# A one-byte memset on GpSimd after each gather of a two-layer graph network

## The chip, the cores and the metric

The kernel runs on one core of a Trainium2 chip. The metric is the device time of one execution in microseconds. A profile of one execution is given with it; its engines are PE (TensorE's matmuls), PEld (TensorE's weight loads), DVE (VectorE), ACT (ScalarE), POOL (GpSimd) and SP (SyncE, which here only issues DMAs).

## The reference

A relational graph convolution with two layers runs over 12,500 nodes of 128 features and 200,000 edges that are sorted by their destination. Each edge has one of 8 types. In each layer every edge takes its source node's row through its type's 128 x 128 matrix; the messages of one destination and type are averaged, the averages summed over the types, and `x @ root + bias` added. A relu and the layer's input follow. At the end the first input is added and a layer norm taken.

```python
def _rgcn_conv(x, src, dst, et, basis, comp, root, bias):
    W = jnp.einsum('rb,bio->rio', comp, basis)
    xw = jnp.einsum('ni,rio->nro', x, W)
    msgs = xw[src, et]
    seg = dst * N_REL + et
    summed = jax.ops.segment_sum(msgs, seg, num_segments=N_NODES * N_REL)
    cnt = jax.ops.segment_sum(jnp.ones((msgs.shape[0],), x.dtype), seg, num_segments=N_NODES * N_REL)
    mean = summed / jnp.maximum(cnt, 1.0)[:, None]
    agg = mean.reshape(N_NODES, N_REL, HIDDEN).sum(axis=1)
    return agg + x @ root + bias
...
for l in range(N_LAYERS):
    h_new = jax.nn.relu(_rgcn_conv(h, src, dst, edge_type, basis[l], comp[l], root[l], bias[l]))
    h = h_new + h
...
x = _layernorm(x + h, axis=-1)
```

## The kernel before

The edges are cut into T = 1563 tiles of 128. A *quad* is Q = 4 tiles (391 quads in a layer), a *group* is 8 tiles. One indirect DMA on GpSimd (`gather`, line 577) fetches the 128 source rows of one tile from HBM, 64 KB, into a quarter of a `rows` buffer. The `rows` buffers form a ring of AHEAD + 2 = 14 quads, so 56 gathers fit; the loop issues the gathers of quad q + 12 when it writes the code of quad q.

In layer 1 the rows come from `x`. For each quad VectorE builds one-hot matrices `dm` weighted with the inverse counts (`onehot`, line 863), TensorE multiplies `rows` by `dm` into `s` (`means`, line 903), and ScalarE copies `s` from PSUM to `sT` (line 565 is the helper of all its copies). Each group then goes through the eight type matrices into `y` (`product`, line 927), ScalarE copies that to `ys`, and TensorE puts it in its place (`place`, line 950). A finished block of 128 nodes is turned and multiplied by all eight matrices of layer 2 (`close_block`, lines 963 to 975), and SP stores the products to `y_d`.

In layer 2 the rows come ready multiplied from `y_d`. So a quad needs only `dm` and one product per tile, accumulated in PSUM over the quads of a block (`add_rows`, line 1016). `finish` and `norm` (lines 1028 to 1057) add bias, relu, residual and layer norm on VectorE and ScalarE, and SP stores the block. Layer 2's first gather waits for the last store of `y_d`. At the start of layer 1 VectorE and TensorE also count the edges of each destination and type (`counts`, lines 699 to 706).

A planner (`Plan`) takes the operations in the order written and gives each engine its waits on semaphores. Each engine runs its own operations in that order. A quad's gathers wait for TensorE to have used the ring's buffer 14 quads before, and for the quad three before to have landed, since the quads take turns on three DMA semaphores (`"gq": 3`). TensorE's products wait for the landing and for `dm`. A second, general path in the file runs only if the edges do not fit the assumptions of the first; it does not run here.

Of the kernel before, what the change touches and what calls it, by code (L numbers as in the profile page):

```python
# [415 lines left out]
def ordered_path(  # L416
# [24 lines left out]
    nc = tc.nc  # L441
    P = 128
    N, D = x.shape
    E = src.shape[0]
    L, NB = basis.shape[0], basis.shape[1]
# [3 lines left out]
    T = -(-E // P)  # L449
# [4 lines left out]
    Q = 4  # L454
# [16 lines left out]
    def keep(shape, dtype, name):  # L471
        return const.tile(shape, dtype, name=name)

    hT_d = dram.tile([NT * P, P], F32, name="hT_d")
    y_d = dram.tile([N * R, D], F32, name="y_d")
# [28 lines left out]
    sel = keep([P, G, K], F32, "sel")  # L504
    spread = keep([P, B, GB], F32, "spread")

    key = keep([P, 4, C], F16, "key")
    low = keep([P, 4, C], I32, "low")
    eqs = Ring(const, 2, [P, S4, 4, C], F16, "eq")
# [59 lines left out]
    def gather(l, q):  # L569
        if q >= NQ:  # L570
            return
        t, cell = rows_r.take()
        rows_g[l, q] = (t, cell)
        ids = idx if l == 0 else idy

        def emit():
            return [nc.gpsimd.indirect_dma_start(  # L577
                out=t[:, i - q * Q, :], out_offset=None, in_=x if l == 0 else y_d,
                in_offset=bass.IndirectOffsetOnAxis(ap=ids[:, i:i + 1], axis=0))
                for i in range(q * Q, min((q + 1) * Q, T))]  # L580

        b = q * Q // P
        reads = ["idx0" if l == 0 and q == 0 else ("idx", b)] if l == 0 else [("idy", b)]
        if l == 1 and q == 0:
            reads += [("y_d", j) for j in range(NT)]
        plan.add("POOL", emit, reads, [cell], lane="gq", n=min(Q, T - q * Q))
# [590 lines left out]
@with_exitstack  # L1177
def kernel(
    ctx: ExitStack,
    tc: tile.TileContext,  # L1180
    x: bass.AP,
    src: bass.AP,
    dst: bass.AP,
    et: bass.AP,
    basis: bass.AP,
    comp: bass.AP,
    root: bass.AP,
    bias: bass.AP,
    out: bass.AP,
):  # L1190

    nc = tc.nc
    flag = ctx.enter_context(tc.tile_pool(name="flag", bufs=1))
    bad = flag.tile([1, 1], I32, name="bad")
    ordered_path(tc, bad, x, src, dst, et, basis, comp, root, bias, out)
    redo = nc.values_load(bad, min_val=0, max_val=P_MAX)  # L1200
    with tc.If(redo > 0):
        general_path(tc, x, src, dst, et, basis, comp, root, bias, out)
# [27 lines left out]
```

## Time and profile before

| | |
|---|---|
| median of 3 runs | 4643.5 us (4638.13 to 4643.62) |
| the profiled execution's own time | 4641.11 us |
| its span in the profile | 4639.3 us |
| busy: PE, PEld, DVE, ACT, POOL | 51%, 41%, 37%, 11%, 64% |
| gathers | 3126: layer 1 starts from 3.4 to 2327.4 us, layer 2 from 2379.7 to 4590.5 us |
| DMA packets | all queues together took 22% of the 16 engines, mean 64 GB/s |
| granted TensorE clock, mean | 0.776 |

A line of the profile's groups gives the source line, the engine, the operation, what it writes and reads and how often; then the busy time in us and the mean length of one in ns; then the engine's idle time ahead of these instructions and what ended most of it. "Issue" there is time in which the engine waited for nothing that the profile shows, and "remote" is a wait whose end the profile can't ascribe to an instruction. A line of the list of waits gives the total in us, the number of waits and the longest. A line of the timeline gives the start in us, the length in us, the engine, the line and the operation; behind it in brackets stands the idle time ahead of it. TensorE runs each float32 matmul in two records, so a quad's four products are eight records.

### The profile page before, as it was taken

To read this page: it belongs to the slowest core of one execution; us is meant where nothing else is said; L and a number is where in the kernel's file an instruction comes from. 1 tells how busy PE (TensorE), PEld (TensorE's weight loads), DVE (VectorE), ACT (ScalarE), POOL (GpSimd) and SP (SyncE) were. 2 spreads that over 40 slices of the span, in tenths; PEclk is the share of its full clock that TensorE was granted. 3 is DMA by queue.
4 is the path that set the end of the run, shared out by engine and by line. 5 is a ranking of instruction groups with operands and counts; after the bars stand their busy time and mean duration, and the time that the engine had idled before them with its cause. 6 is when DMAs were issued, how large, how long until landed. Compare 5 with 4: busy or idle time off the path is not lost.

```text
span 4639.3 us, 34983 instructions
## 1 busy us (share of the span) xinstructions
PE 2355.8 (51%) x11691; PEld 1911.0 (41%) x11691; DVE 1697.2 (37%) x4724; ACT 502.0 (11%) x1190; POOL 2962.0 (64%) x3134
## 2 busy tenths in 40 slices
PE   1675565556655565565563443444444344444444
PEld 1454555455544554454442332333333233333333
DVE  3874222222222232232232343434334343434434
ACT  0121111111111111121110000000000000000000
POOL 5466666666666666666646666666666666666663
PEclk9998888788788877788876776777777776767677
DMA  2122222222222222222221111211111111111121
GB/s 79 37 71 74 75 75 74 74 75 75 74 74 74 75 79 73 72 79 74 70 69 51 55 56 54 57 55 56 54 56 56 55 56 56 54 55 56 54 57 37
DMA packets 193392, 295.75 MB, mean 64 GB/s; under 512 B 60725, under 2 KB 130687, under 8 KB 193203
## 3 DMA queue, kind: packets, MB, share of 16 engines
q0 software_dynamic: 100032, 205.07, 15.6%
q1 hardware_dynamic: 90650, 86.62, 5.8%
q8 instruction: 96, 1.57, 0.1%
q10 hardware_dynamic: 2521, 1.73, 0.1%
q14 instruction: 93, 0.76, 0.1%
HBM read 229.18 MB, written 64.00 MB: 63 GB/s over the span
## 4 chain that ended last, share of the span: by engine, by line
another core or an unknown queue 38%; PE 26%; DVE 17%; issue 14%; ACT 3%; POOL 2%; DMA 0%; POOLq 0%; DVEq 0%; ACTq 0%; SPq 0%
DVE dm L863 12%; PE s L903 8%; PE y L927 6%; PE pt L975 4%; PE po L950 3%; POOL rows L577 2%; PE s L1016 1%; ACT sT L565 1%; DVE w_sb L597 1%; PE ct L705 1%; DVE eq L699 1%; PE ct L706 1%; DVE st L1052 1%; DVE ys L1057 1%
## 5 line engine op out<-in xcount | busy, mean ns | idle before, releaser
L577 POOL DMA_INDIRECT rows<-in_x_dram,idx x1563 | 1485.4, 950 | 841.0 <-issue 420.5
L577 POOL DMA_INDIRECT rows<-y_d,idy x1563 | 1475.5, 944 | 787.6 <-issue 419.0
L1016 PE MATMUL s<-dm,rows 128*128 128x256 f32 x2086 | 646.0, 469 | 595.1 <-DVE dm L863 482.0
L863 DVE TENSOR_SCALAR dm<-cols,near,w 128x256 f32<-128x256 f32 x1563 | 727.0, 533 | 255.3 <-remote 185.9
L1016 PEld LDWEIGHTS s<-dm,rows 128*128 128x128 f32 x2086 | 487.6, 245 | 710.3 <-DVE dm L863 499.6
L863 DVE TENSOR_SCALAR dm<-cols,kr,w 128x128 f32<-128x128 f32 x1563 | 525.9, 401 | 569.3 <-remote 348.1
L903 PEld LDWEIGHTS s<-dm,rows 128*128 128x128 f32 x3126 | 470.9, 222 | 121.9 <-issue 115.4
L903 PE MATMUL s<-dm,rows 128*128 128x128 f32 x3126 | 485.5, 305 | 6.1 <-issue 5.1
L950 PE MATMUL po<-ys,pl 128*128 128x128 f32 x780 | 167.6, 349 | 628.3 <-ACT ys L565 467.6
L927 PE MATMUL y<-w_sb,sT 128*128 128x128 f32 x3136 | 439.5, 300 | 65.4 <-issue 43.3
L1016 PE MATMUL ct<-dm,rows 128*128 128x256 f32 x1040 | 314.6, 457 | 291.1 <-DVE dm L863 216.7
L927 PEld LDWEIGHTS y<-w_sb,sT 128*128 128x128 f32 x3136 | 422.8, 216 | 75.1 <-issue 48.8
L950 PEld LDWEIGHTS po<-ys,pl 128*128 128x128 f32 x780 | 131.1, 239 | 656.4 <-ACT ys L565 486.9
L1016 PEld LDWEIGHTS ct<-dm,rows 128*128 128x128 f32 x1040 | 235.2, 237 | 347.7 <-DVE dm L863 224.7
L963 DVE TENSOR_TENSOR h<-po,bias_sb 128x128 f32<-128x128 f32 x98 | 28.5, 291 | 872.3 <-PE s L903 281.2
L1051 DVE TENSOR_TENSOR h<-po,xs 128x128 f32<-128x128 f32 x98 | 27.9, 285 | 816.6 <-remote 731.7
L565 ACT ACTIVATE sT<-s 128x512 f32<-128x512 f32 x391 | 233.8, 598 | 838.5 <-PE s L903 466.3
L975 PE MATMUL pt<-w_sb,y_col 128*128 128x512 f32 x392 | 254.1, 736 | 55.2 <-issue 31.2
L1050 PE MATMUL po<-ident,y_col 128*128 128x128 f32 x98 | 37.5, 383 | 379.8 <-DVE y_col L1036 185.3
L1050 PEld LDWEIGHTS po<-ident,y_col 128*128 128x128 f32 x98 | 15.4, 157 | 415.2 <-DVE y_col L1036 205.8
L1054 ACT ACTIVATE st<-st,eps 128x1 f32<-128x1 f32 x98 | 28.9, 294 | 1187.8 <-DVE st L1053 931.6
L565 ACT ACTIVATE y_row<-pt 128x512 f32<-128x512 f32 x196 | 117.0, 597 | 215.0 <-PE pt L975 95.2
(120 smaller groups left out, 1148.9 us busy)
## 6 DMA issues: line engine op xcount, KB each, us to landing
y_d<-y_row SPq DMA_DIRECT2D x97, 512.0 KB
rows<-in_x_dram,idx POOLq DMA_INDIRECT x1563
rows<-y_d,idy POOLq DMA_INDIRECT x1563
h_in<-in_x_dram SPq DMA_DIRECT2D x98, 64.0 KB
h_in<-hT_d SPq DMA_DIRECT2D x98, 64.0 KB
xs<-in_x_dram SPq DMA_DIRECT2D x98, 64.0 KB
hT_d<-y_col SPq DMA_DIRECT2D x97, 64.0 KB
out_dram<-ys SPq DMA_DIRECT2D x97, 64.0 KB
```

The source lines that it names most:

```text
L565: act(lambda: nc.scalar.activation(out_t, in_t, AF.Copy), reads, writes)
L577: return [nc.gpsimd.indirect_dma_start(out=t[:, i - q * Q, :], out_offset=None, in_=x if l == 0 else y_d, in_offset=bass.IndirectOffsetOnA ...
L597: vec(lambda b=b: nc.vector.scalar_tensor_tensor(w_sb[:, l, r, :], b_sb[:, l, b, :], comp_sb[:, c0 + b:c0 + b + 1], w_sb[:, l, r, :], op0= ...
L699: vec(lambda s=s, eq=eq, s0=s0: nc.vector.tensor_tensor(eq[:, s - s0, :nb, HALO - s:HALO + P], key[:, :nb, HALO - s:HALO + P], key[:, :nb, ...
L705: nc.tensor.matmul(ct[:, :nb, :], id_h, eq[:, s - s0, :nb, main], start=(s == 1), stop=False)
L863: last = nc.vector.tensor_scalar(t[:, i - q * Q, :wide], cols[:, :wide], ids[:, i:i + 1], w[:, i:i + 1], op0=ALU.is_equal, op1=ALU.mult)
L903: last = nc.tensor.matmul(s[:, i, :], t[:, i, :], d[:, i, :P], start=True, stop=True)
L927: last = nc.tensor.matmul(y[:m], t[:, r, :nt, :].rearrange("p t k -> p (t k)"), w_sb[:, 0, r, :], start=(r == 0), stop=(r == R - 1))
L950: last = nc.tensor.matmul(po[j][0][:n], t[:m, k * P:k * P + n], o[:m], start=False, stop=(j in closed))
L975: pe(lambda: nc.tensor.matmul(pt[:n].rearrange("p r d -> p (r d)"), yc[:, :n], w_sb[:, 1, k * H:(k + 1) * H, :].rearrange("p r d -> p (r d)"),
L1016: ins = nc.tensor.matmul(a, t[:, i, :], d[:, i, :], start=(opens and i == 0), stop=(last and i == n - 1))
L1050: pe(lambda: nc.tensor.transpose(p[:n, :], v[:, :n], ident), [vc, "ident"], [pc])
```

## The change

A scratch tile `pace` of one byte per partition and gather is added. After each gather, GpSimd clears that gather's byte in all 128 partitions. The planner still sees only the gathers: the memset has no wait and signals nobody.

```diff
+    pace = keep([P, L * T], mybir.dt.uint8, "pace")
...
         def emit():
-            return [nc.gpsimd.indirect_dma_start(
-                out=t[:, i - q * Q, :], out_offset=None, in_=x if l == 0 else y_d,
-                in_offset=bass.IndirectOffsetOnAxis(ap=ids[:, i:i + 1], axis=0))
-                for i in range(q * Q, min((q + 1) * Q, T))]
+            ins = []
+            for i in range(q * Q, min((q + 1) * Q, T)):
+                ins.append(nc.gpsimd.indirect_dma_start(
+                    out=t[:, i - q * Q, :], out_offset=None, in_=x if l == 0 else y_d,
+                    in_offset=bass.IndirectOffsetOnAxis(ap=ids[:, i:i + 1], axis=0)))
+                nc.gpsimd.memset(pace[:, l * T + i:l * T + i + 1], 0)
+            return ins
```

## The prediction

> **What bounds the kernel now.** I read the costliest groups first. GpSimd issues 3126 gathers, 1563 per layer:
>
> ```profile
> L577 POOL DMA_INDIRECT rows<-in_x_dram,idx x1563 | 1485.4, 950 | 841.0 <-issue 420.5 <-PE s L903 195.9 <-remote 186.9
> L577 POOL DMA_INDIRECT rows<-y_d,idy x1563 | 1475.5, 944 | 787.6 <-issue 419.0 <-remote 243.0 <-DMA y_d<-y_row 51.4
> ```
>
> A gather is busy for 0.944 us, and half of the idle time ahead of it is "issue", which is no wait: GpSimd's timeline has the next gather 0.30 us after the last one's end, so the undisturbed beat is 1.249 us. 3126 x 1.249 = 3904 us of the 4639.3 us span. No other engine is busy for more than 51%, so the rest is not somebody else's work; it is pauses of this chain. By first and last starts (3.4 and 2327.4 us; 2379.7 and 4590.5 us) layer 1 takes 2324.0 us where 1562 beats are 1951, layer 2 takes 2210.8. So 373 us of pauses lie in layer 1, 260 in layer 2; beside them stand 3.4 us at the start, 51 between the layers and 48 after the last gather. Of the 373, 103 fall before 331 us, where only 180 gathers were issued and VectorE is 70 to 80% busy counting edges. About 530 us of pauses are left for the steady part.
>
> GpSimd's list of waits tells for whom it pauses:
>
> ```profile
> POOL rows L577 <- remote: 429.9, 145, 11.3
> POOL rows L577 <- PE s L903: 195.9, 74, 31.4
> ```
>
> The wait is the one for TensorE to free the `rows` buffer of 14 quads ago. So TensorE seems late. But a window without gathers (between the layers) says that it is not slow. Here are ScalarE's copies of `s`, one per quad, with the gathers and without; the columns are the stretch, its length, ScalarE's busy time and count, the clock, the DMA share:
>
> ```profile
> 350.00:2320.00 1970.00, 203.77 (x341) 0.81 0.25 74
> 2332.00:2376.00 44.00, 7.06 (x12) 0.97 0.19 70
> ```
>
> With gathers a quad takes 1970 / 341 = 5.78 us. Without them 44 / 12 = 3.67, where four gathers need 5.0. What holds TensorE up is seen in the timeline of all engines:
>
> ```profile
> 1503.19 0.94 POOL L577 DMA_INDIRECT rows<-in_x_dram,idx  x1 [0.30 <-issue]
> 1503.63 0.27 PE L903 MATMUL s<-dm,rows 128*128 128x128 f32 x1 [0.27 <-issue]
> 1506.48 0.60 ACT L565 ACTIVATE sT<-s 128x512 f32<-128x512 f32 x1 [5.08 <-remote]
> 1506.71 0.94 POOL L577 DMA_INDIRECT rows<-in_x_dram,idx  x1 [2.58 <-remote]
> ```
>
> TensorE's last product of the quad ends at 1503.9 us; ScalarE, idle, may copy it only at 1506.48, 2.6 us later and 2.3 us after GpSimd fell silent. GpSimd's own wait, also for TensorE, ends 0.2 us after that. The start of the program shows the same with no ring and no gathered data in play: VectorE's comparison waits for TensorE while gathers stream without a break.
>
> ```profile
> 51.30 0.69 DVE L699 TENSOR_TENSOR eq<-key 128x157 f16<-128x157 f16 x4 [20.95 <-remote]
> ```
>
> So my reading is: **while gathers follow each other at 1.25 us, TensorE's completions reach the other engines late, often only when GpSimd pauses; the ring then fills, GpSimd pauses, and everything comes free.** GpSimd's beat is the floor; these late completions are what stands on top of it. Why they are late, the trace does not say.
>
> **What the Trainium skill says.** "Perfetto Trace Analysis", section "GPSIMD Engine Instruction", advises timing GpSimd's instructions by start-to-start spacing and not by the reported span. The trace agrees: the only memsets of 128x1 that GpSimd runs are reported with 99 to 119 ns and start 30 ns apart:
>
> ```profile
> 0.30 0.11 POOL L1216 MEMSET const-bfloat16-1.0<- 128x1 bf16 x1
> 0.33 0.12 POOL L1216 MEMSET const-uint8-127<- 128x1 uint8 x1
> ```
>
> "GPSIMD Engine Reference", section "2.1 Instruction dispatch": completion of an instruction holds back who waits on its semaphore, not the next GpSimd instruction. The memset has no semaphore, so by this the next gather need not await its write; these overlapping memsets agree. "SBUF — State Buffer", section "Who interferes with whom": a VectorE instruction with two SBUF inputs contends with a GpSimd instruction that reads SBUF, not with one that only writes. A memset only writes; whether it collides, no run here shows. "Perfetto Trace Analysis", section "Tensor Engine Instruction": TensorE's reported end is estimated and its semaphore follows PSUM's acknowledgement. So a late completion could be real work behind a modelled end. Against that stands the window between the layers, where ScalarE's 11 waits for `s` come to 5.1 us in all.
>
> **The change part by part.** It removes and moves nothing: the compiled order of PE, DVE, ACT and SP is the same instruction by instruction, and no wait is added. It adds 3126 memsets on GpSimd, each behind a gather. Behind each stands the next gather; VectorE, ScalarE and SP do not wait for it. The new tile is written by nobody else.
>
> Price of one, d. Lower bound 0.03 us (the spacing). Upper bound 0.40 us: its 0.10 us, and a gap of 0.30 of its own as between two gathers. I take 0.10 us, its reported length, since nothing overlaps a gather here today and a memset would run in the gap at best. A beat becomes 1.349 us. There are 2 x 1562 = 3124 beats, so 312 us more on GpSimd.
>
> It lies beside the pauses, of which there are 633 us; it is hidden only as far as these shrink. If completions come in time, the sum is: 3124 x 1.349 = 4214; start, middle and end 3.4 + 51 + 48 = 102; start-up pauses 103 less the 180 x 0.10 = 18 that the longer beat eats, 85; a tenth of the steady pauses left, 53, as I do not expect all to go. That is 4454 us. Less some of the middle and the end, which now hold up to 14 quads of backlog: 11 fewer quads at 3.67 us (layer 1) and at 2.2 us (layer 2, 90 matmul records of 8 per quad in 25 us after the last gather) would save 64; I count half, 32. So 4422 us of span. The profiled execution took 4641.1 us, its span 4639.3, and the median of the three runs is 4643.5, 4 us above the span: **about 4430 us**, 4.6% less. Late next would be GpSimd itself, with TensorE a few quads behind it.
>
> The step that I can't derive is that 0.10 us between gathers is enough. For it: the lateness is seen only in streams of gathers at the short beat, and completions within a stream do get through, some after 1 us and some after 14 us, so it is a matter of chance slots and not a lock; and the steady pauses of 530 us are worth more than 312. Against it: within a stream most beats let none through, and a memset keeps GpSimd as busy as before.
>
> **The rivals.**
> 1. *The holds stay and the beat adds up (slower).* If completions still come mainly in the pauses, each turn of the ring, 12 gathers and a pause of 2.6 us (1506.71 to 1524.07 us), gets 12 x 0.10 longer and its pause stays. Then 4643.5 + 312 - 18 = 4938 us. For it: at the pause of 1521.4 us the same 2.4 us pass before TensorE is heard. Against it: 3.67 us per quad as soon as gathers stop. It decides if under 312 of the 633 us of pauses go.
> 2. *The memset is dear (slower).* With no steady pauses at all, GpSimd alone reaches today's span where 102 + 85 + 3124 x (1.249 + d) = 4639, that is at d = 0.176 us. At the upper bound of 0.40 it is 102 + 85 + 3124 x 1.649 = 5339 us. For it: the constant 0.30 us between gathers could be a cost of every instruction there. Against it: the 30 ns between memsets, and iotas that start 0.08 to 0.31 us apart without such a gap.
> 3. *No change.* Either the memset runs inside the 0.30 us and the beat stays (it doesn't do what it says), or holds last a fixed time and the pauses shrink by just what the beats gain: 4640 us.
>
> **How the numbers follow.** A measurement of this kernel can tell about 0.2% (9 us) from no change. Forecast 0.52, rival 1 0.27, rival 2 0.13, rival 3 0.08. Faster 0.52, same 0.08, slower 0.40. Low end: the forecast at d = 0.03 is 3124 x 0.07 = 219 less, 4211; I put 4220. High end: rival 1 at d = 0.13 is 4643.5 + 406 - 23 = 5027; 5050 leaves out most of rival 2 and the dear end of rival 1, some 0.15. Where the signs split so, the likeliest case's own range is 4220 to 4600.
>
> **What would show it.** Right: GpSimd's starts 1.33 to 1.37 us apart in both layers; its waits for TensorE and "remote" down from 626 us to under 150; ScalarE's copies of `sT` and VectorE's L1051 without waits of 5 us and more; the gathers of a layer spread over some 2110 to 2230 us. Wrong: a start-to-start of 1.45 us or more (rival 2); pauses of 2.6 us that still come every 8 to 12 gathers behind the longer beat (rival 1); starts still 1.25 us apart (rival 3).

## The result, and the profile after

The change makes no gain: 4655.8 us after (median of 10 runs, 4652.7 to 4662.1) against 4645.4 us before (10 runs, 4636.7 to 4650.7), a ratio of 1.0024 with a 95% interval of 1.0015 to 1.0034. Faster by 4.6% was forecast; it is slower by a quarter of a per cent. The memset is there, 3126 times, and the beat is what it was.

These are the costliest groups of GpSimd in the profile after (busy us, mean ns, idle time ahead and what ended it). Lines of the kernel have moved by 3 or 4 against those of before:

```profile
L580 POOL DMA_INDIRECT rows<-in_x_dram,idx x1563 | 1488.1, 952 | 659.5 <-issue 268.9
L580 POOL DMA_INDIRECT rows<-y_d,idy x1563 | 1476.8, 945 | 612.6 <-issue 296.5
L583 POOL MEMSET pace<- 128x1 uint8 x3126 | 375.0, 120 | 4.2 <-issue 2.5
```

The memsets are busy for 375 us, the 312 us of the forecast and more. But the "issue" ahead of the gathers fell from 839.5 us (420.5 + 419.0) to 565.4. The memset took the place of idle time. GpSimd's timeline shows how (start, length, and in brackets the idle time ahead):

```profile
1502.47 0.94 POOL L580 DMA_INDIRECT rows<-in_x_dram,idx  x1 [0.19 <-issue]
1503.41 0.12 POOL L583 MEMSET pace<- 128x1 uint8 x1
1503.71 0.94 POOL L580 DMA_INDIRECT rows<-in_x_dram,idx  x1 [0.19 <-issue]
1504.66 0.12 POOL L583 MEMSET pace<- 128x1 uint8 x1
1504.96 0.94 POOL L580 DMA_INDIRECT rows<-in_x_dram,idx  x1 [0.19 <-issue]
```

The memset starts as the gather ends, lasts 0.12 us, and the next gather follows 0.19 us behind it: 1502.47, 1503.71, 1504.96, still 1.25 us apart. The median over all gathers is 1.250 us, against 1.249.

With the beat the pauses stayed too. The waits of GpSimd for a `rows` buffer (total us, number, longest):

```profile
POOL rows L580 <- remote: 422.5, 164, 5.0
POOL rows L580 <- PE s L907: 157.5, 59, 31.3
```

That is 580 us where before had 626. The total is less in part because the memset now fills 0.12 us of each wait. Measured from start to start, less 1562 beats, the pauses did not shrink: 376 us in layer 1 and 264 in layer 2, against 373 and 260. ScalarE's copies of `s` come at the pace of before, 1970 us for 342 of them (before 341):

```profile
350.00:2320.00 1970.00, 204.57 (x342) 0.80 0.26 75
```

The two profiled spans, 4654.8 and 4639.3 us, differ by 15.5 us: 4.8 in layer 1 (first to last gather 2328.8 against 2324.0), 5.2 between the layers (57.5 against 52.3), 5.4 in layer 2 (2216.2 against 2210.8), nothing after the last gather. These are two single executions, and executions of one kernel differ by as much (4636.7 to 4650.7 us before), so the split is only a rough one.

### The profile page after: what moved, and what is told of

Read it like the earlier page. It is cut to its first block, busy times and chain, and to the rows that moved or that the text cites. A ratio compares the mean times of both kernels' runs of the same rounds, so it can differ in the third digit from the quotient of the medians.

```text
span 4654.8 us, 38109 instructions
## 1 busy us (share of the span) xinstructions
PE 2351.6 (51%) x11691; PEld 1909.1 (41%) x11691; DVE 1700.7 (37%) x4724; ACT 503.6 (11%) x1190; POOL 3330.0 (72%) x6260
## 4 chain that ended last, share of the span: by engine, by line
another core or an unknown queue 39%; PE 25%; DVE 15%; issue 13%; POOL 4%; ACT 3%; DMA 0%; ACTq 0%; POOLq 0%; DVEq 0%; SPq 0%
DVE dm L867 10%; PE s L907 7%; PE y L931 5%; PE pt L979 4%; POOL rows L580 4%; PE po L954 3%; PE s L1020 3%; PE ct L1020 1%; ACT sT L566 1%; DVE w_sb L601 1%; PE ct L709 1%; DVE eq L703 1%; PE ct L710 1%; DVE st L1056 1%
## 5 line engine op out<-in xcount | busy, mean ns | idle before, releaser
L1020 PE MATMUL s<-dm,rows 128*128 128x256 f32 x2086 | 619.6, 455 | 480.5 <-DVE dm L867 252.2
L583 POOL MEMSET pace<- 128x1 uint8 x3126 | 375.0, 120 | 4.2 <-issue 2.5
L1054 PEld LDWEIGHTS po<-ident,y_col 128*128 128x128 f32 x98 | 15.5, 158 | 619.3 <-DVE y_col L1040 382.6
```

The lines of the kernel that those rows point to most:

```text
L583: nc.gpsimd.memset(pace[:, l * T + i:l * T + i + 1], 0)
L1020: ins = nc.tensor.matmul(a, t[:, i, :], d[:, i, :], start=(opens and i == 0), stop=(last and i == n - 1))
L1054: pe(lambda: nc.tensor.transpose(p[:n, :], v[:, :n], ident), [vc, "ident"], [pc])
```

## The experiments

The theories have letters in the expectations. For the price of the memset: **A**, a gather has a turn-round of 0.305 us in which GpSimd has room for a short instruction; **C**, each instruction adds its time to the beat. For the late completions: **B**, a longer beat relieves them and the time is 187 + 3124 x beat (187 us are the start, middle, end and start-up pauses of the forecast), as the forecast had it; **C'** (rival 1), the pauses stay on top; **D** (the second half of rival 3), a longer beat is absorbed; **F**, they belong to the chip or its surroundings; **G**, they belong to the rhythm of the program. Each group of runs has its own runs of the kernel before on the same chip. The kernels that take rows by SP ran once on each chip, and in them the values are not the reference's.

### How long a memset the turn-round hides

Four variants of the change: one memset of 256 or of 512 bytes, four of one byte, and one of one byte per quad instead of per gather. The wide ones write a ring of four quads and wait for the memsets of four quads ago, long done.

```diff
-    pace = keep([P, L * T], mybir.dt.uint8, "pace")
+    pace = keep([P, 4, Q, 256], mybir.dt.uint8, "pace")          # or 512
...
-                nc.gpsimd.memset(pace[:, l * T + i:l * T + i + 1], 0)
+                nc.gpsimd.memset(pace[:, (l * NQ + q) % 4, i - q * Q, :], 0).then_inc(paced, 1)
```
```diff
+    pace = keep([P, 4 * L * T], mybir.dt.uint8, "pace")           # four
...
-                nc.gpsimd.memset(pace[:, l * T + i:l * T + i + 1], 0)
+                for c in range(4):
+                    k = 4 * (l * T + i) + c
+                    nc.gpsimd.memset(pace[:, k:k + 1], 0)
```
```diff
-                nc.gpsimd.memset(pace[:, l * T + i:l * T + i + 1], 0)
+            i = q * Q                                             # one per quad, behind its gathers
+            nc.gpsimd.memset(pace[:, l * T + i:l * T + i + 1], 0)
```

> The memset after each gather clears 256 bytes per partition instead of one. Theory A (turn-round): the 0.30 us between two gathers is GpSimd's own turn-round, and an instruction shorter than that runs inside it; a memset of 256 elements should last about 0.3 us (the iota of 256 elements took 0.34), so the beat should be 1.25 to 1.40 us. Theory B (relief, the forecast's): with a beat b the late completions of TensorE go away and the time is about 187 + 3124 b, so 4250 to 4560 us. Theory C (adding up): the pauses stay and the time is about 4645 + 3124 (b - 1.25), so up to 5110 us. Theory D (absorbed): the pauses shrink by what the beats gain, 4645 us as long as 3124 (b - 1.25) is under some 500 us.

> The memset after each gather clears 512 bytes per partition. By the iotas it should last about 0.55 us, more than the 0.30 us between gathers, so the beat should be 1.5 to 1.8 us. B (relief): 187 + 3124 b, 4870 us at b = 1.5. C (adding up): 4645 + 3124 (b - 1.25), 5430 us at b = 1.5. D (absorbed): as B once the pauses are used up, but with pauses of 2.6 us still seen below that point.

> Four one-byte memsets after each gather instead of one, each on a byte of its own. If memsets follow each other at 30 ns as at the program's start, the four end 0.21 us after the gather and the beat stays 1.25 us: 4645 to 4670 us by theory A. If each takes its 0.12 us in turn, 0.48 us, the beat is 1.45 us or more: B 4720 us, C 5270 us.

> One one-byte memset per quad of four gathers, behind the fourth. If the change's 10 us (0.24%) come from each memset (2.5 ns each), this costs a quarter, 2 to 3 us. If they come from the pattern of waits having shifted, the time may be anything within 0.3% of before. If they come from a fixed cost such as the larger program, it is nearly the whole 10 us only if that does not scale with the count.

Two things came out. The first is the size of the room:

| after each gather | memset, us | beat, us | time, us | ratio to before |
|---|---|---|---|---|
| nothing (before) | | 1.249 | 3994.2 | |
| one byte, once per quad | 0.12 | 1.249 | 3995.3 | 1.0002 (0.9994 to 1.0011) |
| four of one byte, 28 ns apart | 0.20 together | 1.294 | 4135.5 | 1.0355 (1.0340 to 1.0371) |
| 256 bytes | 0.325 | 1.441 | 4573.5 | 1.1449 (1.1431 to 1.1467) |
| 512 bytes | 0.538 | 1.654 | 5239.8 | 1.3120 (1.3100 to 1.3140) |

GpSimd's timeline with 256 bytes shows the rule. The memset starts with the gather's end, and the gather follows 0.17 us after the memset's:

```profile
1499.44 0.95 POOL L584 DMA_INDIRECT rows<-in_x_dram,idx  x1 [0.17 <-POOL pace L587]
1500.38 0.34 POOL L587 MEMSET pace<- 128x256 uint8 x1
1500.88 0.95 POOL L584 DMA_INDIRECT rows<-in_x_dram,idx  x1 [0.16 <-issue]
```

All rows fit one sentence: a gather starts at the later of 0.305 us after the last gather's end and 0.165 us after the last memset's end (0.149 behind four). So 0.14 us are free, and the change's memset of 0.12 fits with 0.02 to spare. (In the kernels with wide memsets, which also signal a semaphore, the gather itself lasts 0.950 us instead of 0.944.) Beyond the room every 0.01 us costs 31 us: the four memsets lengthen the beat by 0.045, x 3124 = 141 us, and 141 was measured.

C falls: it asks for a beat of 1.249 + 0.325 = 1.574 us with 256 bytes. A holds only with a smaller room than it was given. It had taken the whole 0.30 us for free, and so expected 1.25 us behind four memsets and at most 1.40 with 256 bytes; both were missed. The 0.14 us were fitted to these runs, and the sizes below test them.

The second was not expected: the kernel before took 3994 us on this chip, not 4645. So the run with one memset per quad, which was to tell where the change's loss of 10 us comes from, could not: on this chip there is no loss to divide.

### The same two programs on a chip without late completions

Before and the change once more on another chip; with them a kernel whose rows come by plain transfers of SP and which has no gathers, and one with SP's rows and, beside them, all gathers into a ring of their own that nobody reads.

```diff
-                nc.gpsimd.indirect_dma_start(out=t[:, i - q * Q, :], ...)
+                r0 = i * P % (N - P) if l == 0 else i * P % (N * R - P)
+                ins.append(nc.sync.dma_start(t[:, i - q * Q, :], (x if l == 0 else y_d)[r0:r0 + P, :]))
...
+        dt_, dc_ = dummy_r.take()                                 # the second kernel only
+        plan.add("POOL", beat, reads, [dc_], lane="gq", n=min(Q, T - q * Q))
```

> The kernel before once more, for a trace on the same chip as the other runs of this group. Theory A (turn-round) says nothing on its time. Theory F (the late completions belong to the chip or its surroundings, not to the program) expects either about 4645 us with pauses of some 630 us and waits of 5 us and more for TensorE, or about 3994 us with 22 + 22 us between and after the layers and next to no pauses, and nothing between. Theory G (they belong to the program's rhythm of gathers) expects 4645 us on any chip.

> The changed kernel once more. Theory A: a one-byte memset ends 0.12 us after the gather and the next gather can follow 0.17 us later, inside the 0.30 us, so the beat stays within 2 ns of 1.249 us. Where there are no pauses this gives before + 0 to 6 us (0 to 0.15%); where there are pauses the same plus what their pattern does, up to 15 us. The forecast's step (the memset costs 0.10 us of beat) would give 312 us more where there are no pauses.

> The rows are loaded by plain DMAs from SP, 128 rows that lie together for each tile, instead of being gathered; GpSimd issues nothing. So the rows are not the ones of the edges, and the output differs. If GpSimd's gathers are the floor, the time falls to what TensorE, VectorE and ScalarE need: by the windows without gathers 391 x 3.67 + 391 x 2.2 us and some 150 us at the ends, about 2450 us. If the late completions come from DMA traffic in general, waits for TensorE of over 3 us are seen here too; if from GpSimd's gathers, none.

> As the run with rows from SP, and GpSimd issues all 3126 gathers of before into a scratch ring that nobody reads (waiting only for their own landings). So the output differs, and the gathers never pause for TensorE. GpSimd needs 3126 x 1.25 = 3905 us by itself. If an unbroken stream of gathers delays TensorE's completions, the waits for TensorE grow far past those of before (14 to 21 us at the start of before) and the time lies well over 4000 us. If TensorE is delayed only by something else, the time is about 3905 us or what the stores add, and TensorE keeps ahead of the gathers.

Before took 3995.7 us here and the change 3995.9, a ratio of 1.0001 (0.9992 to 1.0009). So where nothing is late, the memset is free within 0.1%. These are GpSimd's waits in the kernel before, on this chip; "remote" is gone from the list, and in its place stand start-up waits and the store of `y_d`:

```profile
POOL rows L577 <- issue: 911.5, 2991, 0.5
POOL rows L577 <- PE s L903: 38.4, 24, 7.1
POOL rows L577 <- DMA y_d<-y_row: 20.5, 1, 20.5
```

Gather (0.944 us) and beat (1.249) are those of the first profile; the spans differ by 644.9 us, of which 592.7 are pauses (632.9 less 40.2), 30.9 the middle (52.3 less 21.4) and 21.5 the end (48.8 less 27.3). Without gathers the rest of the kernel takes 2160 us (about 2450 had been expected), so the gathers are the bound on this chip. With unread gathers it took 3940.5 us, without late completions although GpSimd never pauses. Here the stream alone delays nothing. F holds so far; what a longer beat does where completions are late could not be seen on such a chip.

The granted clock is also lower in the first profile of before, 0.776 on average against 0.82 here. It does not explain the 645 us: TensorE's products of `rows` are not longer there. The first line is from the first profile, the second from this chip:

```profile
L903 PE MATMUL s<-dm,rows 128*128 128x128 f32 x3126 | 485.5, 305 | 6.1 <-issue 5.1
L903 PE MATMUL s<-dm,rows 128*128 128x128 f32 x3126 | 506.3, 312 | 542.6 <-DMA rows<-in_x_dram,idx 541.5
```

In the second, TensorE waits for gathered rows, as it should where the gathers are the bound.

### Two sizes between, for the beat of the forecast

> One memset of 64 bytes after each gather, in a ring of four quads, else as the change. From the memsets of 1, 256 and 512 bytes (0.12, 0.325, 0.538 us) this one should take 0.12 + 63 x 0.00083 = 0.17 us at most (under 0.12 if short ones have a floor). Turn-round with room (A): the next gather starts 0.166 us after the memset or 0.305 after the gather, whichever is later: beat 0.944 + 0.17 + 0.166 = 1.280 us. Adding up (C): 1.249 + 0.17 = 1.419. On a chip without late completions, where the kernel before takes 3994: A gives 3994 + 3124 x 0.031 = 4091, C 4525. On a chip with them, where it takes 4645: relief (B) gives 187 + 3124 x 1.280 = 4186 under A, faster than before; if the pauses stay, 4645 + 97 = 4742.

> As the run with 64 bytes, with 128: memset 0.12 + 127 x 0.00083 = 0.225 us at most. A: beat 0.944 + 0.225 + 0.166 = 1.335 us, close to the 1.349 on which the forecast rested; C: 1.474. On a chip where the kernel before takes 3994: A gives 3994 + 3124 x 0.086 = 4263. On one where it takes 4645 with late completions: relief (B) gives 187 + 3124 x 1.335 = 4358, faster than before by 6%; if the pauses stay beside the longer beat, 4645 + 269 = 4914.

As the kernel with 256 bytes, with 64 and 128. The chip was again one where before takes 3995.1 us. Memsets of 0.165 and 0.218 us gave beats of 1.280 and 1.334, and 4088.6 us (1.0234, 1.0217 to 1.0251) and 4254.8 us (1.0650, 1.0632 to 1.0667). A, with the room of 0.14 us, had said 4091 and 4263. The lengths of the memsets are the profile's own, but the beats alone say the same: from 64 to 512 bytes they grow by 0.00083 us per byte, and carried down, this line meets the beat without a memset (0.950 + 0.305 us) near 34 bytes. That is an estimate from these beats; one byte lies well inside.

### A chip with late completions: a full room, and a short ring

As above with 32 bytes; and the kernel before with `AHEAD = 4`, a ring of 6 quads instead of 14.

> One memset of 32 bytes after each gather, in a ring of four quads: by the runs with 64, 128 and 256 bytes (0.168, 0.221, 0.325 us) it takes 0.142 us. Turn-round with room (A): the next gather starts at the later of 0.305 us after the gather and 0.166 us after the memset, which here is 0.308: a beat of 1.252 us, the size at which the room is just full. On a chip where the kernel before takes 3995: A gives 3995 to 4010, C (adding up) 4438. On a chip with late completions, where it takes 4645: still about 4645 if the beat rules nothing there; relief (B) as the forecast had it needs a longer beat than this and is tested by the other sizes only.

> The kernel before with a ring of 6 quads of rows instead of 14 (AHEAD = 4 instead of 12), no memset. The gathers then meet full buffers sooner. On a chip without late completions (before 3995), if the ring's depth covers only the start-up and small unevenness: 4000 to 4100, pauses for TensorE below 100 us. If even there the depth hides delays of 10 us and more at each norm or layer step: 4200 or more. On a chip with late completions (before 4645), pauses grow from 630 us to well over 1000: over 5000.

This chip had before at 4641.5 us. With 32 bytes: memset 0.143, beat 1.258, 4656.4 us, a ratio of 1.0031 (1.0020 to 1.0043). The beat grew by 0.009, 28 us in all, and not by the 0.003 expected: the memset still fits (0.143 + 0.165 = 0.308), but the gather itself lasted 0.953 us. Against the first profile of before, the pauses shrank by 18 (363 and 252 us against 373 and 260) and the layers grew by only 10. That speaks for D, but the step is small.

The short ring was expected to cost hundreds of us and **gained**: 4608.5 us, 0.9930 (0.9913 to 0.9946). By first and last gathers, layer 1 takes 2327.3 us (before, in the first profile, 2324.0), layer 2 2207.3 (2210.8): between 6 and 14 quads, the depth doesn't matter to the steady part. The middle shrinks from 52.3 to 37.2 and the end from 48.8 to 36.3, as one would expect if fewer quads wait in the ring when the gathers stop. +3.3 - 3.5 - 15.1 - 12.5 = -27.8, and the spans differ by 27.7. My expectation took the ring for a cushion; where the engines behind are the slower side, a longer ring is only a longer queue.

### Five beats and none, in one run

To be independent of the luck of the chip, one kernel takes all beats through: per layer six stretches of about 65 quads.

```diff
+    width = lambda l, q: (0, 64, 128, 256, 512, -1)[(q if l == 0 else NQ - 1 - q) * 6 // NQ]
...
+            if wide < 0:                                          # rows by SP, no gathers
+                ...
+                if wide:
+                    nc.gpsimd.memset(pace[:, n % 4, i - q * Q, :wide], 0).then_inc(paced, 1)
```

> One kernel with six stretches of about 65 quads in each layer (layer 2 in the reverse order): after each gather no memset, one of 64, of 128, of 256, of 512 bytes, and in the last stretch no gathers at all, the rows coming by plain transfers of SP from consecutive rows (there the values are not the reference's). Read is the time per tile of 128 rows in each stretch, after its first 16 quads. On a chip without late completions: the beats of the model, 1.249, 1.280, 1.334, 1.441, 1.654, and about 0.69 without gathers (2160 / 3126). On a chip with them (1.442 per tile in layer 1 and 1.417 in layer 2 of the kernel before, pauses counted): relief (B), 1.44, 1.28, 1.33, 1.44, 1.65; pauses stay on top of the beat (C'), 1.44, 1.47, 1.53, 1.63, 1.85; the engines behind the gathers have a rate of their own, whatever the beat (D), 1.44, 1.44, 1.44, 1.45, 1.65, and then also about 1.44 without gathers if they are slow by themselves, or clearly less if the gathers slow them.

> The kernel with six stretches once more, on another chip. Without late completions (kernel before 3995): 4022, as measured. With them (kernel before 4645), per tile of 128 rows in the stretches none, 64, 128, 256, 512 bytes: relief (B) 1.44, 1.28, 1.33, 1.44, 1.65; pauses on top (C') 1.44, 1.47, 1.53, 1.63, 1.85; a rate of their own (D) 1.44, 1.44, 1.44, 1.45, 1.65. Without gathers: 0.67 as on the chip just seen if the gathers cause the delays, about 1.44 if the engines behind them are slow by themselves, in between if both.

The first run fell on a chip where before takes 3996.9 us, and gave the beats of A (4021.7 us). The second fell on one where it takes 4640.1, and took 4303.3, one execution each. Time per tile after the first 16 quads of a stretch, by the starts of the gathers (without gathers, by VectorE's `dm`, after 14 quads):

| after each gather | chip without late completions, layers 1, 2 | chip with them, layers 1, 2 |
|---|---|---|
| nothing | (start-up), 1.249 | (start-up), 1.411 |
| 64 bytes | 1.280, 1.280 | 1.445, 1.429 |
| 128 bytes | 1.335, 1.335 | 1.445, 1.417 |
| 256 bytes | 1.442, 1.443 | 1.442, 1.443 |
| 512 bytes | 1.655, 1.655 | 1.655, 1.655 |
| no gathers | 0.645, 0.583 | 0.645, 0.584 |

In the first profile of before, layer 1 runs at 1.44 per tile after its first fifth and layer 2 at 1.41 to 1.42. So on the late chip a beat of 1.28 or 1.33 changes nothing; one of 1.44 is level with the rate, and only one of 1.65 sets it. These are windows of GpSimd's gathers in layer 1 for 64, 128, 256, 512 bytes, then in layer 2 for 128 and 64 (stretch, length, busy and count, clock, DMA share, GB/s):

```profile
550.00:830.00 280.00, 184.09 (x194) 0.80 0.24 74
930.00:1200.00 270.00, 176.81 (x186) 0.77 0.25 75
1300.00:1580.00 280.00, 184.48 (x194) 0.77 0.24 72
1680.00:2010.00 330.00, 189.43 (x200) 0.80 0.25 75
3240.00:3510.00 270.00, 181.10 (x191) 0.70 0.19 54
3610.00:3880.00 270.00, 179.72 (x189) 0.72 0.19 55
```

280 / 194 = 1.44, 270 / 186 = 1.45, 1.44, 1.65; 270 / 191 = 1.41, 270 / 189 = 1.43. And this is VectorE's `dm`, one per tile, in the stretch without gathers, 130 / 203 = 0.64:

```profile
2040.00:2170.00 130.00, 67.68 (x203) 1.00 0.52 159
```

D holds against B and C' at 64 and 128 bytes; at 256 and 512, B and D ask for the same. The pauses give way as the beat grows: counting starts that come over 0.3 us behind the beat, after a stretch's first gathers, layer 1 has 23 of them in 243 gathers with 64 bytes, 15 in 240 with 128 and none in 242 with 256. What sets the rate of 1.44 us no run shows. The delays themselves: the waits put down to "remote", summed over all engines, are 258, 147 and 263 us in layer 1's stretches of 64, 128 and 256 bytes, and 2.6 in that of 512. In layer 2, which comes to them from the slow end, 512 and 256 bytes have none and 128 bytes have 270. So relief exists, but it starts between 1.334 and 1.443 us in layer 2 and above 1.442 in layer 1, where the beat is as long as what it relieves. (The stretches run in opposite orders, so the layer and what went before it are not told apart.) With 256 bytes GpSimd never pauses in layer 1 and the engines behind keep up all the same: pauses are not the only thing that lets completions out. And the last row: the same engines, on the same chip, in the same run, are as quick as elsewhere as soon as no gathers run.

### Is it the stream of gathers alone?

The kernel with SP's rows and unread gathers again, until a chip with late completions came.

> The kernel whose rows come by plain transfers of SP from consecutive rows, while GpSimd runs all 3126 gathers into a scratch ring that nobody reads (the values are not the reference's), on one more chip. GpSimd never waits for TensorE here, so it has no pauses. Without late completions (kernel before 3995): 3940, as measured, the engines behind running at about 0.67 us per tile. With them (kernel before 4645): if the stream of gathers itself delays TensorE's completions, the engines behind take 1.3 us per tile or more, stay level with the gathers or fall behind them, and the end comes after 3940, at 4300 to 4600; if it needs TensorE to work on gathered rows, 3940 and 0.67 us per tile.

> The kernel with SP's rows and 3126 unread gathers again, on another chip. Without late completions: 3940 to 3945, 0.67 us per tile behind the gathers. With them (kernel before 4645): 1.3 us per tile or more and an end at 4300 to 4600 if the stream of gathers itself delays TensorE's completions; 3940 and 0.67 us per tile if it needs TensorE to work on gathered rows.

> The kernel with SP's rows and 3126 unread gathers, a last time on another chip. As before: without late completions 3940 to 3945; with them (kernel before 4645) 1.3 us per tile or more behind the gathers and 4300 to 4600 if the stream of gathers itself delays TensorE's completions, 3940 if not.

Twice it fell on chips where before takes 3994 and 3993 us, and took 3945.1 and 3942.9. The third time, on the chip of the second run with six stretches (before 4639.6), it took **6096.0 us**, far over the 4300 to 4600 that I had put down. Here are TensorE and GpSimd in 40 slices of that span, busy tenths:

```profile
PE   0110101010011159999981111110111111168887
POOL 7677777777777710000007777777777777700000
```

While the gathers run without a pause, TensorE all but stands; when they stop, it is at once fully busy. (They stop in the middle because layer 2's first gather waits 1010 us for the last store of `y_d`.) Windows of `dm` in the four parts (stretch, length, busy and count, clock, DMA share, GB/s): 22.5 us per tile (1800 / 80), 0.65, 6.0, 0.59.

```profile
300.00:2100.00 1800.00, 26.98 (x80) 0.53 0.20 51
2200.00:3150.00 950.00, 486.35 (x1455) 1.00 0.54 162
3300.00:5300.00 2000.00, 154.94 (x332) 0.56 0.23 60
5480.00:6060.00 580.00, 456.01 (x987) 1.00 0.46 131
```

The sheer amount of transfers is not what stalls TensorE: the two quick parts move the most, 162 and 131 GB/s against 51 and 60. The list of waits between 300 and 2100 us, total, number and longest:

```profile
ACT sT L566 <- remote: 1084.2, 19, 77.8
DVE eq L710 <- remote: 814.0, 10, 116.1
DVE h L974 <- remote: 512.7, 4, 143.1
```

And the timeline shows how little gets through. For a while TensorE's loads and products stand alone, 0.40 us after a gather's start, one per gather:

```profile
1046.65 1.09 POOL L592 DMA_INDIRECT dummy<-in_x_dram,idx  x1 [0.30 <-issue]
1047.05 0.37 PE L914 MATMUL s<-dm,rows 128*128 128x128 f32 x1 [2.43 <-issue]
1048.05 1.09 POOL L592 DMA_INDIRECT dummy<-in_x_dram,idx  x1 [0.30 <-issue]
1048.45 0.29 PEld L914 LDWEIGHTS s<-dm,rows 128*128 128x128 f32 x1 [2.51 <-issue]
1049.45 1.09 POOL L592 DMA_INDIRECT dummy<-in_x_dram,idx  x1 [0.30 <-issue]
1049.85 0.37 PE L914 MATMUL s<-dm,rows 128*128 128x128 f32 x1 [2.43 <-issue]
```

This pattern is not the rule of the whole stretch: between 300 and 2100 us TensorE runs 1291 loads and products beside 1295 gathers, one per gather on average, but 914 gathers see none, 248 see one, and 41 see ten or more. Nor is it the clock, 0.53 there: a product lasts 0.37 us, and TensorE is idle for 2.4 us before the next.

So on this chip the stream of gathers holds TensorE and its completions back, whether or not anybody reads what is gathered. It needs such a chip, as F says (the chip or its surroundings: no run tells which), and it needs the stream; G's 4645 us on any chip is refuted. Three quarters of the gathers in that stretch grew from 0.944 to about 1.095 us, and with them the beat to 1.400. That beat relieves nothing here, while 1.44 with a memset of 256 bytes did let the work through; no run tells the longer beat from the memset in it. In the kernel before, the ring is what saves TensorE: it runs full, GpSimd has to pause, and the pause lets the completions out.

## Why the prediction was wrong

**The reading of the profile was right for that chip.** "While gathers follow each other at 1.25 us, TensorE's completions reach the other engines late, often only when GpSimd pauses" is what the kernel with unread gathers shows: waits whose longest last 78 to 143 us while no pause comes. (One side reading was off: before 331 us VectorE is 62% busy, and 70% and more only after the first 100 us. Nothing in the sum rests on it.) What no single profile could tell is that the 633 us of pauses were not the program's: on two of the eight chips of the experiments before takes 4640 to 4642 us, on six 3993 to 3997. (Which chip the first result came from is not on record.)

**"Price of one, d ... I take 0.10 us" is the first step that failed.** The lengthening measured is 0.001 us on the chip with late completions and none on the other; "starts still 1.25 us apart", which the prediction had named as rival 3's sign, is what the profile shows. The text put the memset "in the gap at best" and then added its length to the beat all the same. If it runs in the gap, it must be asked how much of the gap is free; the answer is 0.14 of 0.305 us, and the memset takes 0.12. Even the lower bound of 0.03 excluded this: it was made from the spacing of memsets among each other, which says nothing of what follows a gather. (The prediction took from "GPSIMD Engine Reference", section "2.1 Instruction dispatch", that the next gather need not await the memset's write. It waits on no semaphore of it, but in every run with memsets of 0.165 us and more it started 0.16 to 0.17 us after the memset's reported end, and 0.149 behind four that signal nobody: free of the write, perhaps, but not of the instruction.) So about 3 of the 312 us came on GpSimd, and 4454 was the sum of a kernel that didn't exist.

**The relief, the step that "I can't derive", failed as well.** The change never tried it; the six stretches did. At 1.334 us, near the 1.349 of the forecast, the late chip ran at 1.445 and 1.417 per tile, as with no memset. So had the price been 0.10 us, the time would by these rates have been about that of before, not 4430. The argument for it, that completions within a stream do get through by chance slots, missed that the pauses are not a surcharge on a beat: they shrink as the beat grows, and the rate per tile stays. Relief was right in kind and wrong in size: it takes a beat of about 1.44 us, where nothing is left to gain.

**The rivals.** Rival 1 falls by the same table: nothing is added, 1.445 where it needs 1.53. Rival 2 needs a memset of 0.176 us on the beat, and 0.001 was measured. Rival 3 is right in the outcome of both halves, which it gave as alternatives: the memset runs inside the 0.30 us, and a longer beat, up to 1.44 us, is absorbed (though not by holds of a fixed time: the pauses become fewer). It had a chance of 0.08 and 4640 us; the measured 4655.8 lies 16 above it. The chance I gave it was too small. The 0.305 us stood in the profile as time in which GpSimd waited for nothing, and idle time that an instruction could use deserved to be the likeliest case, not the last.

**The small loss stays open.** The 10 us (0.24%) are beyond chance, came again with 32 bytes (0.31%), and are absent where nothing is late (0.01%, -0.08 to 0.09%). In the two traces they lie in both layers and between them. It would fit that a busier GpSimd holds completions back a little longer, but no run separates that from the extra instructions themselves. Why one chip holds TensorE back behind gathers and another doesn't is open too; in before and in the change, the lengths of gather (0.944 and 0.945 us) and memset (0.12) are the same on both.

## What to carry to other kernels

Before an instruction is added between two of a kind, split the idle time between those two into what the engine needs and what is free: here 0.14 of 0.305 us were free, a memset of 0.12 us cost next to nothing and one of 0.165 cost 0.031 per gather. Where an engine pauses because a ring is full, compute the rate from pause to pause (1.44 us per tile) and try it as the bound: here beats below it moved nothing, and a shallower ring changed only the ends. And before a stall in a trace is priced, see whether the program has it on a second chip: here it was 650 of 4645 us.

## What was not expected of the hardware

- The same program takes 3993 to 3997 us on six chips and 4640 to 4642 on two, with the same length of its gathers (0.944 us) and the same beat (1.249) in the two profiles kept.
- On one chip of the second kind, in one execution, beside a stream of gathers without pauses TensorE ran 1291 loads and products in 1800 us, one per gather on average, and completions came up to 143 us late; three quarters of the gathers grew to about 1.095 us. On three chips of the first kind the same program is not delayed (3940 to 3945 against 6096 us).
- Lengths of a memset of 128 partitions on GpSimd: 0.12, 0.143, 0.165, 0.218, 0.325 and 0.538 us for 1, 32, 64, 128, 256 and 512 bytes; four of one byte start 28 ns apart.
